# Inverse deviations of the norms by a logarithm and an exponential on ScalarE in place of a power on GpSimd, in a four-layer graph network kernel

## The chip, the cores and the metric

The kernel runs on one core of a Trainium2 chip. A core has five engines that run side by side, each with its own in-order queue of instructions: TensorE (PE, matrix products; its weight loads are shown apart as PEld), VectorE (DVE), ScalarE (ACT), GpSimd (POOL) and SyncE (SP), which here issues the DMAs. The metric is the device time of one execution in microseconds (us), lower is better. A profile page and the answers of the trace come from one profiled execution.

## The reference, cut to what matters

The input `x` is 32 batches of 512 nodes with 128 features; `adj` is a 512 x 512 adjacency matrix of zeros and ones. Four graph layers follow each other, each as a residual around a layer norm without weights:

```python
def _layernorm(x, axis=-1, eps=1e-5):
    m = jnp.mean(x, axis=axis, keepdims=True)
    v = jnp.var(x, axis=axis, keepdims=True)
    return (x - m) / jnp.sqrt(v + eps)

h = jnp.maximum(_layernorm(x), 0.0); x = x + layer0(h, adj)   # pair attention
h = jnp.maximum(_layernorm(x), 0.0); x = x + layer1(h, adj)   # attention, norm, adjacency sum, MLP with a norm
h = jnp.maximum(_layernorm(x), 0.0); x = x + layer2(h, adj)   # attention, elu
h = jnp.maximum(_layernorm(x), 0.0); x = x + layer3(h, adj)   # softmax of a learned adjacency
return x
```

So each batch needs six norms: one ahead of each layer and two inside layer 1 (one after its attention, one in its MLP). Every norm needs one inverse deviation, 1/sqrt(v + eps), for each of the 512 nodes. The 512 nodes lie as 4 chunks of 128 partitions, so that the inverse deviations of one norm are a 128 x 4 tile. 32 batches make 192 norms.

## The kernel before

**How the work is cut.** The unit is one batch in one layer, a 128 x 4 x 128 tile in float32. `xs` holds `x` for all batches in on-chip memory from load to store. `layer0(b)` to `layer3(b)` record the operations of one batch: the norm (`preln`), a projection, attention scores, and products that accumulate in PSUM banks. All matrix work is float32 on PE.

**What sets the order.** The kernel doesn't issue instructions as it records them. Each operation is handed to a planner (`Plan`) with its engine, an estimated length in us and the values that it reads and writes. Each batch in each layer is a chain with a due time: the layers of successive batches start at the distances `GAPS`, and layers 1, 2 and 3 of a batch follow 6, 12 and 16 batches behind layer 0 (`LAGS`). `Plan.run` then goes through all operations once, always takes the one that can begin first by the estimated lengths (ties within 0.05 us go to the earlier due time), and emits it. The order that comes out is fixed for each engine. So a change to the engine or length of one kind of operation moves the order of all engines.

**Idle products.** Where the planner finds PE without work for more than 0.6 us and a PSUM bank is free, it emits dummy transposes of the identity matrix, one for every 0.11 us of the gap beyond 0.2 us (`idle_products`, L334). They keep PE busy and compute nothing that is used. The program before has 150 of them.

**A norm, step by step.** `variances` (L511, L513, VectorE) gives mean and variance, `mv`. `inv_dev` gives `rstd`: on GpSimd, `ve = mv + eps` (L523), then `ve` to the power -0.5 (L525). Ahead of layer 0 of the first eight batches (`EARLY`) the normalized tile `xn` is made on ScalarE (L545); in all other norms ahead of a layer it is made on GpSimd in four pieces (L560), with the negated mean, `shift`, from ScalarE (L556). PE turns `xn` into `pt` (L421), and ScalarE copies that to `hT` with the ReLU (L570). In layer 1 the norm after the attention takes its power at L892 from a `ve` that VectorE makes (L883), and VectorE uses it in `hn` (L899); the norm of the MLP uses `inv_dev`, and ScalarE scales `zn` by it (L927).

**Small tiles** (`mv`, `rstd`, `shift` and the like) come from the pool `sm` with eight buffers for each name.

**DMA.** SP issues the loads of `x` (L405), the rearranged scores `u` of layer 0 (L699) and the stores of the result (L992), in the planner's order.

The power itself is two lines:

```python
nc.gpsimd.tensor_scalar(ve, mv.own[:, :, 1], LN_EPS, 1.0, ALU.add, ALU.mult)
nc.gpsimd.tensor_tensor(rstd.own, ve, mhalf, ALU.pow)
```

Of the kernel before, what the change touches and what calls it, by code (L numbers as in the profile page):

```python
# [28 lines left out]
F32 = mybir.dt.float32  # L29
# [4 lines left out]
AF = mybir.ActivationFunctionType  # L34
ALU = mybir.AluOpType
# [9 lines left out]
OLD, KEPT = 4, 1  # L45

AHEAD = 6


PE, DVE, ACT, POOL, SP = "PE", "DVE", "ACT", "POOL", "SP"  # L50
# [207 lines left out]
def kernel(  # L258
# [33 lines left out]
    P2 = P + 2  # L292
    NE = l3_e.shape[1]
    KE = NE // P
    assert F == P and C == 4 and NE % P == 0 and B >= AHEAD

    cp = ctx.enter_context(tc.tile_pool(name="const", bufs=1))
    ps = ctx.enter_context(tc.tile_pool(name="ps", bufs=8, space=bass.MemoryType.PSUM))
    sm = ctx.enter_context(tc.tile_pool(name="sm", bufs=8))

    def wide(t):

# [4 lines left out]

    def small(name, shape=(P, C)):
        return sm.tile(list(shape), F32, name=name, tag=name)

    def const(name, shape, dtype=F32):
        return cp.tile(list(shape), dtype, name=name)
# [40 lines left out]
    nc.vector.memset(mhalf, -0.5)  # L353
    minus1 = const("minus1", (P, 1))
    nc.vector.memset(minus1, -1.0)
    one_b = const("one_b", (P, 1), BF16)
    nc.vector.memset(one_b, 1.0)


    xs = const("xs", (P, B, C, P))  # L360
    W_S, W_2, W_30, W_31 = range(4)
    wts = const("wts", (P, 4, P))
    att = const("att", (P, 2))
# [30 lines left out]
    def row_of(n):  # L394
        return rows[:, n : n + 1, :].to_broadcast([P, C, P])

    v_x = [Value() for _ in range(B)]
    v_adj = [Value() for _ in range(C)]
    v_adjT = [Value() for _ in range(C)]
    v_biasT, v_mask2T, v_cnt, v_w0, v_wts = Value(), Value(), Value(), Value(), [Value() for _ in range(4)]  # L400
# [3 lines left out]
    def load(dst, src, writes, size=0.0):  # L404
        op(SP, 0.5, lambda: nc.sync.dma_start(dst(), src), writes=writes, load=size, transfers=1)  # L405

    def load_x(b):
        load(lambda: xs[:, b], x[b].rearrange("(c p) f -> p c f", p=P), [v_x[b]], 1.0)

    def copy_op(engine, length, dst, src, reads, writes):  # L410
        if engine is ACT:
# [88 lines left out]
    def dve(length, emit, reads, writes, port=0):  # L500
        op(DVE, length, emit, reads, writes, port=port)

    def variances(src, reads):

        mv = Value()

        def emit():
            st = small("st", (P, C, 6))
            mv.own = small("mv", (P, C, 2))
            for c in range(C):  # L510
                nc.vector.bn_stats(st[:, c, :], src(c))  # L511
            for c in range(C):
                nc.vector.bn_aggr(mv.own[:, c, :], st[:, c, :])  # L513

        dve(1.1, emit, reads, [mv])
        return mv

    def inv_dev(mv):
        rstd = Value()

        def emit():
            ve = small("ve")
            nc.gpsimd.tensor_scalar(ve, mv.own[:, :, 1], LN_EPS, 1.0, ALU.add, ALU.mult)  # L523
            rstd.own = small("rstd")
            nc.gpsimd.tensor_tensor(rstd.own, ve, mhalf, ALU.pow)  # L525

        op(POOL, 1.3, emit, [mv], [rstd])
        return rstd

    def preln(b, engine):  # L530

        src = xs[:, b]
        mv = variances(lambda c: src[:, c, :], [v_x[b]])
        rstd = inv_dev(mv)
        shift = Value()
        xn = value(by_act if engine is ACT else by_pool, "xn")
        if engine is ACT:

            def emit_shift():
                shift.own = small("shift")  # L540
                nc.vector.scalar_tensor_tensor(shift.own, mv.own[:, :, 0], -1.0, rstd.own, ALU.mult, ALU.mult)

            def norm():
                for c in range(C):
                    nc.scalar.activation(  # L545
                        xn.t[:, c, :], src[:, c, :], AF.Identity, bias=shift.own[:, c : c + 1],
                        scale=rstd.own[:, c : c + 1],
                    )

            dve(0.08, emit_shift, [mv, rstd], [shift], port=1)  # L550
            op(ACT, 1.54, norm, [shift, rstd, v_x[b]], [xn])
        else:

            def emit_shift():
                shift.own = small("shift")
                nc.scalar.mul(shift.own, mv.own[:, :, 0], -1.0)  # L556

            def norm():
                for c in range(C):
                    nc.gpsimd.tensor_scalar(  # L560
                        xn.t[:, c, :], src[:, c, :], shift.own[:, c : c + 1], rstd.own[:, c : c + 1],
                        ALU.add, ALU.mult,
                    )

            op(ACT, 0.1, emit_shift, [mv], [shift])
            op(POOL, 1.72, norm, [shift, rstd, v_x[b]], [xn], port=4)
        pt = value(banks, "pt")
        turn_op(lambda k: pt.t[:, k, :], lambda k: xn.t[:, k, :], [xn], [pt])
        hT = value(by_act, "hT")
        op(ACT, 0.49, lambda: nc.scalar.activation(wide(hT.t), wide(pt.t), AF.Relu), [pt], [hT])  # L570
        return hT, pt
# [115 lines left out]
    def layer0(b):  # L687
# [138 lines left out]
        def terms():  # L826
            return second[0].t.rearrange("p (c t) f -> p c t f", c=H)

        for ib in range(C):
# [20 lines left out]
               [hT, v_wts[W_S], *([*y, hs] if ib < H else [v_mask2T, *hi, *lo])], [po[ib]])  # L850
        rest = value(by_act, "rest")
        op(ACT, 0.27, lambda: nc.scalar.copy(rest.t[:, 0:H, :], terms()[:, :, 1, :]), second, [rest])
        dve(0.33, lambda: nc.vector.tensor_add(xs[:, b, 0:H, :], xs[:, b, 0:H, :], first[0].t[:, 0:H, :]),
            first, [v_x[b]])
        dve(0.33, lambda: nc.vector.tensor_add(xs[:, b, H:, :], xs[:, b, H:, :], terms()[:, :, 0, :]),
            second, [v_x[b]])
        op(POOL, 0.7, lambda: nc.gpsimd.tensor_add(xs[:, b, H:, :], xs[:, b, H:, :], rest.t[:, 0:H, :]),
           [rest], [v_x[b]], port=1)


    def layer1(b):
# [23 lines left out]
        dve(0.08, emit_q, ssum, [q], port=1)  # L885
        mv = variances(lambda c: po[0].t[:, c, :], po)
        dve(0.08, emit_ve, [q, mv], [ve], port=1)
        rr = Value()

        def emit_rr():  # L890
            rr.own = small("rstd")
            nc.gpsimd.tensor_tensor(rr.own, ve.own, mhalf, ALU.pow)  # L892

        op(POOL, 1.0, emit_rr, [ve], [rr])
        hn = value(by_dve, "hn")

        def emit_hn():
# [27 lines left out]
        def emit_zn():  # L925
# [9 lines left out]
        px = project(zT, wts[:, W_2, :], [v_wts[W_2]], "px")  # L935
        res = value(by_dve, "res")
        op(DVE, 0.6, lambda: nc.vector.tensor_add(res.t, px.t, hgb.t), [px, hgb], [res])
        op(DVE, 0.6, lambda: nc.vector.scalar_tensor_tensor(xs[:, b], res.t, 0.0, xs[:, b], ALU.max, ALU.add),
           [res], [v_x[b]], port=1)


    def layer2(b):
        hT, _ = preln(b, POOL)
        h = project_scored(hT, w2_ext, [v_w2])
        po, ssum = attend(h, lambda: h[0].t[:, :, P], h, h, None, None)
        v1 = value(by_dve, "v1")

        rs = Value()

        def emit_rs():  # L950
            rs.own = small("rs")
            nc.vector.reciprocal(rs.own, ssum[0].own)

        dve(0.1, emit_rs, ssum, [rs])
        dve(0.6, lambda: nc.vector.tensor_mul(v1.t, po[0].t, per_chunk(rs.own)), [*po, rs], [v1])  # L955
        op(POOL, 1.25, lambda: nc.gpsimd.tensor_add(v1.t, v1.t, row_of(B_L2)), [v_rows], [v1], port=1)  # L956


        em = value(by_act, "em")
        op(ACT, 0.62, lambda: nc.scalar.activation(em.t, v1.t, AF.Exp, bias=minus1), [v1], [em])  # L960
        op(DVE, 0.6, lambda: nc.vector.scalar_tensor_tensor(em.t, em.t, 1.0, v1.t, ALU.min, ALU.max), [v1], [em], port=1)  # L961
        op(POOL, 1.25, lambda: nc.gpsimd.tensor_add(xs[:, b], xs[:, b], em.t), [em], [v_x[b]], port=1)  # L962


    def layer3(b):
        hT, pt = preln(b, POOL)

        own = value(by_dve, "own")
        op(DVE, 0.6, lambda: nc.vector.scalar_tensor_tensor(wide(own.t), wide(pt.t), 0.0, adiag_rep, ALU.max, ALU.mult),
           [pt, v_adiag_rep], [own])  # L970
        xb = value(by_pool, "xb")
        op(POOL, 1.25, lambda: nc.gpsimd.tensor_add(xb.t, xs[:, b], row_of(B_L3)), [v_x[b], v_rows], [xb], port=1)
        p1 = project(hT, wts[:, W_31, :], [v_wts[W_31]], "p1")
        h1 = value(by_act, "h1")
        copy_op(ACT, 0.49, lambda: h1.t, lambda: p1.t, [p1], [h1])
        po = parts(banks, "po", C)
        for ib in range(C):

            def emit_po(ib=ib):
                nc.tensor.matmul(  # L980
                    po[ib].t[:, ib, :], lhsT=own.t[:, ib, :], rhs=wts[:, W_30, :], start=True, stop=False
                )
                for jb in range(C):
                    nc.tensor.matmul(  # L984
                        po[ib].t[:, ib, :], lhsT=offT[:, jb, blk(ib)], rhs=h1.t[:, jb, :],
                        start=False, stop=(jb == C - 1),
                    )

            op(PE, 1.11, emit_po, [own, h1, v_offT, v_wts[W_30]], [po[ib]])
        yo = value(by_dve, "yo")  # L990
        op(DVE, 0.6, lambda: nc.vector.tensor_add(yo.t, xb.t, po[0].t), [xb, *po], [yo])
        op(SP, 0.5, lambda: nc.sync.dma_start(out[b].rearrange("(c p) f -> p c f", p=P), yo.t), [yo], [Value()], load=1.0, transfers=1)  # L992
# [369 lines left out]
```

## Time and profile before

| | |
|---|---|
| time, median of 3 runs | 1062.31 us (1062.3 to 1063.7) |
| span of the profiled execution | 1062.1 us |
| mean clock granted to TensorE | 0.996 of full speed |
| power on GpSimd in `inv_dev` (L525) | 160 instructions, 170.9 us busy |
| the addition ahead of it (L523) | 160 instructions, 38.3 us busy |
| power of the norm after the attention (L892) | 32 instructions, 33.6 us busy |
| idle products on PE (L334) | 150 instructions, 19.2 us busy |
| activation table loads on ScalarE | 1, 1.3 us |

How to read the views: the page gives the busy time of each engine and its share of the span. A busy share is an average over stages, so the views by stretch of time give the same for windows that begin and end at chosen microseconds. The chain of waits is followed back from the last instruction: at each step to what released it, or else to the instruction before it on its engine. A group line gives the source line, engine, operation, tiles (out<-in), shape, count, busy time, mean duration in ns, and then the idle time of the engine just before, with what ended it. One float32 product of the source is two PE instructions in the profile; where such instructions follow each other closely their durations overlap, so that a row's busy time can be less than its count times its mean.

### The profile page before, as it was taken

What the parts mean: (1) busy time and instruction counts of PE and PEld (TensorE: products, weight loads), DVE (VectorE), ACT (ScalarE), POOL (GpSimd) and SP (SyncE); (2) the same over time, 40 slices, a digit from 0 to 9 for tenths busy, and PEclk for the clock granted to TensorE, in tenths of its full rate; (3) what the DMA queues carried; (4) which work ended last, traced back from release to release, by engine and by line L of the source; (5) the groups of instructions that cost most, each with busy time, mean ns of one, the idle gap of its engine ahead of it and who ended that gap; (6) DMA issues with size and microseconds to landing.
All of it is one profiled execution on the core that took longest, in us unless ns stands there. A gap on an engine that the chain in (4) does not pass through costs nothing.

```text
span 1062.1 us, 25166 instructions
## 1 busy us (share of the span) xinstructions
PE 1041.7 (98%) x8475; PEld 966.0 (91%) x8475; DVE 868.5 (82%) x3694; ACT 780.5 (73%) x2024; POOL 776.2 (73%) x1140
## 2 busy tenths in 40 slices
PE   7899999999999999999999999999999999999998
PEld 7789789989999999999999999999899999999997
DVE  7799999989988878888888888888888877766752
ACT  6768897789877777777877777787777777767751
POOL 4489577778787777787778778777877666576772
PEclk9899999999999999999999999999999999999999
DMA  6400000000010000000000000000000000000001
GB/s 181 96 12 2 1 2 21 2 12 11 2 31 2 21 21 21 22 21 12 2 12 11 12 12 12 11 2 11 12 11 11 11 11 11 11 22 11 22 24 37
DMA packets 56912, 20.49 MB, mean 19 GB/s; under 512 B 21584, under 2 KB 56272, under 8 KB 56784
## 3 DMA queue, kind: packets, MB, share of 16 engines
q1 hardware_dynamic: 56784, 18.90, 7.2%
q8 instruction: 67, 1.10, 0.5%
q14 instruction: 61, 0.50, 0.2%
HBM read 10.43 MB, written 8.39 MB: 18 GB/s over the span
## 4 chain that ended last, share of the span: by engine, by line
PE 88%; DVE 4%; POOL 3%; DMA 1%; SPq 1%; issue 1%; ACT 1%; POOLq 0%; DVEq 0%; ACTq 0%
PE po L675 20%; PE pt L421 16%; PE po L984 10%; PE pg L911 10%; PE proj L595 7%; PE po L837 5%; PE prow L421 3%; PE p L581 3%; PE pz L581 3%; PE px L581 3%; PE po L980 3%; PE po L842 2%; PE po L834 1%; PE po L847 1%; POOL xn L560 1%
## 5 line engine op out<-in xcount | busy, mean ns | idle before, releaser
L675 PE MATMUL po<-h,pT 128*128 128x128 f32 x2048 | 242.8, 275 | 0.8 <-DVE pT L664 0.8
L675 PEld LDWEIGHTS po<-h,pT 128*128 128x128 f32 x2048 | 236.4, 192 | 5.8 <-issue 4.1
L560 POOL TENSOR_SCALAR xn<-xs,shift,rstd 128x128 f32<-128x128 f32 x480 | 213.1, 459 | 2.8 <-DVE top L633 0.9
L655 ACT ACTIVATE y<-y,nmax 128x512 f32<-128x512 f32 x256 | 181.7, 714 | 5.3 <-DVE nmax L637 4.6
L525 POOL TENSOR_TENSOR rstd<-ve,mhalf 128x4 f32<-128x4 f32 x160 | 170.9, 1068 | 13.3
L622 DVE CUSTOM_DVE_ANT_0 y<-prow,bias 128x512 f32<-128x512 f32 x256 | 162.8, 683 | 1.6 <-PE prow L421 1.6
L984 PE MATMUL po<-h,offT 128*128 128x128 f32 x1024 | 135.4, 275 | 0.0
L911 PE MATMUL pg<-adjTe,hg 128*128 128x512 f32 x256 | 131.0, 593 | 0.0
L421 PE MATMUL pt<-ident,y 128*128 128x128 f32 x1024 | 130.2, 274 | 0.7 <-ACT hl L819 0.7
L421 PEld LDWEIGHTS pt<-ident,y 128*128 128x128 f32 x1024 | 115.1, 141 | 13.8 <-issue 8.5
L984 PEld LDWEIGHTS po<-h,offT 128*128 128x128 f32 x1024 | 124.6, 192 | 0.0
L511 DVE BATCH_NORM_STATS2 st<-xs 128x6 f32<-128x128 f32 x512 | 109.8, 277 | 7.2 <-POOL xs L962 4.5
L595 PEld LDWEIGHTS proj<-w_ext,hT 128*128 128x128 f32 x768 | 96.8, 192 | 19.0 <-issue 9.6
L595 PE MATMUL proj<-w_ext,hT 128*128 128x130 f32 x768 | 102.9, 277 | 1.4 <-ACT hT L570 1.3
L647 ACT ACTIVATE y<-y,src 128x512 f32<-128x512 f32 x128 | 84.6, 714 | 20.8 <-DVE rmax L622 19.6
L962 POOL TENSOR_TENSOR xs<-xs,em 128x512 f32<-128x512 f32 x32 | 42.0, 1312 | 76.8 <-DVE em L961 63.8
L956 POOL TENSOR_TENSOR v<-v,rows 128x512 f32<-128x512 f32 x32 | 40.9, 1279 | 72.4 <-DVE v L955 72.4
L570 ACT ACTIVATE hT<-pt 128x512 f32<-128x512 f32 x128 | 73.5, 589 | 25.3 <-PE pt L421 14.0
L647 ACT ACTIVATE y<-y,h 128x512 f32<-128x512 f32 x128 | 84.7, 714 | 7.9 <-DVE rmax L622 7.7
L664 DVE TENSOR_TENSOR pT<-pt,adjT 128x512 f32<-128x512 f32 x128 | 82.6, 681 | 5.7 <-PE pt L421 5.6
L421 PE MATMUL pt<-ident,xn 128*128 128x128 f32 x512 | 77.8, 274 | 1.5 <-POOL xn L560 1.3
L412 ACT COPY h<-proj 128x260 f32<-128x260 f32 x192 | 66.1, 371 | 13.4 <-PE proj L595 12.4
(204 smaller groups left out, 2302.3 us busy)
## 6 DMA issues: line engine op xcount, KB each, us to landing
xs<-in_x_dram SPq DMA_DIRECT2D x32, 256.0 KB, 4.0
out_dram<-yo SPq DMA_DIRECT2D x32, 256.0 KB, 2.3
u<-h SPq DMA_DIRECT2D x128, 0.5 KB, 1.8
bias<-in_adj_dram SPq DMA_DIRECT2D x4, 256.0 KB, 4.4
wts<-in_L_gnn_W_dram SPq DMA_DIRECT2D x3, 64.0 KB, 4.2
rows<-in_L_gnn_bias_dram SPq DMA_DIRECT2D x2, 64.0 KB, 3.7
wt_o<-L_gnn_others_weight_dram SPq DMA_DIRECT2D x1, 64.0 KB, 2.5
wts<-n_L_gnn_self_weight_dram SPq DMA_DIRECT2D x1, 64.0 KB, 4.5
```

Of the source, the lines that this page charges most:

```text
L421: nc.tensor.transpose(dst(k), src(k), ident)
L511: nc.vector.bn_stats(st[:, c, :], src(c))
L525: nc.gpsimd.tensor_tensor(rstd.own, ve, mhalf, ALU.pow)
L560: nc.gpsimd.tensor_scalar(xn.t[:, c, :], src[:, c, :], shift.own[:, c : c + 1], rstd.own[:, c : c + 1], ALU.add, ALU.mult,)
L581: nc.tensor.matmul(pt.t[:, c, :], lhsT=column(hT, c), rhs=w, start=True, stop=True)
L595: nc.tensor.matmul(p[:, c, :], lhsT=column(hT, 2 * k + c), rhs=w_ext, start=True, stop=True)
L622: nc.vector.tensor_tensor_reduce(wide(y[ib].t), wide(prow.t), bias[:, ib, :], 1.0, LOWEST, ALU.add, ALU.max, rmax.own[:, ib : ib + 1],)
L647: nc.scalar.activation(yw, yw, AF.Prelu, alpha=0.2, bias=src()[:, ib : ib + 1])
L655: nc.scalar.activation(yw, yw, AF.Exp, bias=nmax.own[:, ib : ib + 1], accum_out=ssum[0].own[:, ib : ib + 1])
L675: nc.tensor.matmul(po[ib].t[:, ib, :], lhsT=pT.t[:, jb, :], rhs=h[0].t[:, jb, 0:P], start=(jb == 0), stop=(jb == C - 1),)
L911: nc.tensor.matmul(wide(pg.t), lhsT=hg.t[:, nb, :], rhs=adjTe[:, nb, :], start=(nb == 0), stop=(nb == C - 1))
L984: nc.tensor.matmul(po[ib].t[:, ib, :], lhsT=offT[:, jb, blk(ib)], rhs=h1.t[:, jb, :], start=False, stop=(jb == C - 1),)
```

## The change

The inverse deviation becomes exp(-0.5 * ln(v + eps)) on ScalarE in 184 of the 192 norms: the 152 norms of `inv_dev` outside the first eight of layer 0, and the 32 norms after the attention of layer 1. The first eight norms of layer 0, whose `xn` is made on ScalarE, keep the power on GpSimd. The table set that holds both functions is loaded ahead of the work. `mv`, `rstd`, `shift` and the new `log` tile come from a new pool `sn` with 24 buffers for each name. `xs` holds 26 batches in place of 32, and the last six batches use the room of the first six again.

```diff
+HELD = 26
...
+    sn = ctx.enter_context(tc.tile_pool(name="sn", bufs=24))
...
+    eps_ln = const("eps_ln", (P, 1))
+    nc.vector.memset(eps_ln, LN_EPS)
+    nc.scalar.preload_act_table_set("natural_log_exp_and_others")
...
-    xs = const("xs", (P, B, C, P))
+    xs = const("xs", (P, HELD, C, P))
...
-    v_x = [Value() for _ in range(B)]
+    v_x = [Value() for _ in range(HELD)] * 2
...
-        load(lambda: xs[:, b], x[b].rearrange("(c p) f -> p c f", p=P), [v_x[b]], 1.0)
+        load(lambda: xs[:, b % HELD], x[b].rearrange("(c p) f -> p c f", p=P), [v_x[b]], 1.0)
...
-            mv.own = small("mv", (P, C, 2))
+            mv.own = lasting("mv", (P, C, 2))
...
-    def inv_dev(mv):
+    def inv_root(var, reads, bias=None):
+
+        log, rstd = Value(), Value()
+
+        def emit_log():
+            log.own = lasting("log")
+            if bias is None:
+                nc.scalar.activation(log.own, var(), AF.Ln)
+            else:
+                nc.scalar.activation(log.own, var(), AF.Ln, bias=bias)
+
+        def emit_root():
+            rstd.own = lasting("rstd")
+            nc.scalar.activation(rstd.own, log.own, AF.Exp, scale=-0.5)
+
+        op(ACT, 0.2, emit_log, reads, [log])
+        op(ACT, 0.2, emit_root, [log], [rstd])
+        return rstd
+
+    def inv_dev(mv, engine=ACT):
+        if engine is ACT:
+            return inv_root(lambda: mv.own[:, :, 1], [mv], eps_ln)
         rstd = Value()
...
-        rstd = inv_dev(mv)
+        rstd = inv_dev(mv, POOL if engine is ACT else ACT)
...
-        rr = Value()
-
-        def emit_rr():
-            rr.own = small("rstd")
-            nc.gpsimd.tensor_tensor(rr.own, ve.own, mhalf, ALU.pow)
-
-        op(POOL, 1.0, emit_rr, [ve], [rr])
+        rr = inv_root(lambda: ve.own, [ve])
...
```

More of the change, by code (lines that the diff above doesn't have):

```diff
@@ L294 @@
     KE = NE // P
-    assert F == P and C == 4 and NE % P == 0 and B >= AHEAD
+    assert F == P and C == 4 and NE % P == 0 and AHEAD <= B <= 2 * HELD
     cp = ctx.enter_context(tc.tile_pool(name="const", bufs=1))
@@ L309, in small, with lasting @@
         return sm.tile(list(shape), F32, name=name, tag=name)
+    def lasting(name, shape=(P, C)):
+        return sn.tile(list(shape), F32, name=name, tag=name)
     def const(name, shape, dtype=F32):
@@ L523, in emit @@
             nc.gpsimd.tensor_scalar(ve, mv.own[:, :, 1], LN_EPS, 1.0, ALU.add, ALU.mult)
-            rstd.own = small("rstd")
+            rstd.own = lasting("rstd")
             nc.gpsimd.tensor_tensor(rstd.own, ve, mhalf, ALU.pow)
@@ L530, in preln @@
     def preln(b, engine):
-        src = xs[:, b]
+        src = xs[:, b % HELD]
         mv = variances(lambda c: src[:, c, :], [v_x[b]])
-        rstd = inv_dev(mv)
+        rstd = inv_dev(mv, POOL if engine is ACT else ACT)
         shift = Value()
@@ L539, in emit_shift @@
             def emit_shift():
-                shift.own = small("shift")
+                shift.own = lasting("shift")
                 nc.vector.scalar_tensor_tensor(shift.own, mv.own[:, :, 0], -1.0, rstd.own, ALU.mult, ALU.mult)
@@ L554, in emit_shift @@
             def emit_shift():
-                shift.own = small("shift")
+                shift.own = lasting("shift")
                 nc.scalar.mul(shift.own, mv.own[:, :, 0], -1.0)
@@ L852, in layer0 @@
         op(ACT, 0.27, lambda: nc.scalar.copy(rest.t[:, 0:H, :], terms()[:, :, 1, :]), second, [rest])
-        dve(0.33, lambda: nc.vector.tensor_add(xs[:, b, 0:H, :], xs[:, b, 0:H, :], first[0].t[:, 0:H, :]),
+        dve(0.33, lambda: nc.vector.tensor_add(xs[:, b % HELD, 0:H, :], xs[:, b % HELD, 0:H, :], first[0].t[:, 0:H, :]),
             first, [v_x[b]])
-        dve(0.33, lambda: nc.vector.tensor_add(xs[:, b, H:, :], xs[:, b, H:, :], terms()[:, :, 0, :]),
+        dve(0.33, lambda: nc.vector.tensor_add(xs[:, b % HELD, H:, :], xs[:, b % HELD, H:, :], terms()[:, :, 0, :]),
             second, [v_x[b]])
-        op(POOL, 0.7, lambda: nc.gpsimd.tensor_add(xs[:, b, H:, :], xs[:, b, H:, :], rest.t[:, 0:H, :]),
+        op(POOL, 0.7, lambda: nc.gpsimd.tensor_add(xs[:, b % HELD, H:, :], xs[:, b % HELD, H:, :], rest.t[:, 0:H, :]),
            [rest], [v_x[b]], port=1)
@@ L937, in layer1 @@
         op(DVE, 0.6, lambda: nc.vector.tensor_add(res.t, px.t, hgb.t), [px, hgb], [res])
-        op(DVE, 0.6, lambda: nc.vector.scalar_tensor_tensor(xs[:, b], res.t, 0.0, xs[:, b], ALU.max, ALU.add),
+        op(DVE, 0.6, lambda: nc.vector.scalar_tensor_tensor(xs[:, b % HELD], res.t, 0.0, xs[:, b % HELD], ALU.max, ALU.add),
            [res], [v_x[b]], port=1)
@@ L961, in layer2 @@
         op(DVE, 0.6, lambda: nc.vector.scalar_tensor_tensor(em.t, em.t, 1.0, v1.t, ALU.min, ALU.max), [v1], [em], port=1)
-        op(POOL, 1.25, lambda: nc.gpsimd.tensor_add(xs[:, b], xs[:, b], em.t), [em], [v_x[b]], port=1)
+        op(POOL, 1.25, lambda: nc.gpsimd.tensor_add(xs[:, b % HELD], xs[:, b % HELD], em.t), [em], [v_x[b]], port=1)
     def layer3(b):
@@ L971, in layer3 @@
         xb = value(by_pool, "xb")
-        op(POOL, 1.25, lambda: nc.gpsimd.tensor_add(xb.t, xs[:, b], row_of(B_L3)), [v_x[b], v_rows], [xb], port=1)
+        op(POOL, 1.25, lambda: nc.gpsimd.tensor_add(xb.t, xs[:, b % HELD], row_of(B_L3)), [v_x[b], v_rows], [xb], port=1)
         p1 = project(hT, wts[:, W_31, :], [v_wts[W_31]], "p1")
```

## The prediction

> **What bounds the kernel now.** I read the busy times first, then the chain of waits as shares, then the busy times by stretch, then the chain and the instructions inside the stretches where PE isn't full.
>
> From the page, the busy time of each engine and the chain's shares:
>
> ```profile
> PE 1041.7 (98%) x8475; PEld 966.0 (91%) x8475; DVE 868.5 (82%) x3694; ACT 780.5 (73%) x2024; POOL 776.2 (73%) x1140
> ...
> PE 88%; DVE 4%; POOL 3%; DMA 1%; SPq 1%; issue 1%; ACT 1%; POOLq 0%; DVEq 0%; ACTq 0%
> ```
>
> GpSimd, which the change relieves, holds 3% of the chain; PE holds 88%. By stretch (length, busy time of each engine):
>
> ```profile
> 55.00:74.50 19.50, 17.93 (x148) 16.18 (x148) 18.39 (x88) 10.46 (x38) 16.83 (x26) 1.00 0.05 2
> 74.50:125.40 50.90, 48.86 (x382) 45.03 (x383) 47.93 (x207) 43.31 (x119) 42.86 (x62) 1.00 0.04 7
> 125.40:200.00 74.60, 74.60 (x580) 66.69 (x581) 71.24 (x328) 62.39 (x173) 53.94 (x75) 1.00 0.05 9
> 200.00:985.00 785.00, 784.84 (x6416) 727.56 (x6416) 649.83 (x2692) 591.09 (x1506) 593.35 (x867) 1.00 0.05 13
> 985.00:1062.00 77.00, 71.02 (x624) 69.39 (x622) 39.47 (x122) 35.90 (x79) 42.86 (x63) 0.99 0.08 25
> ```
>
> The reader should see that from 125.4 to 985 us PE is idle for 0.16 us in all. That PE isn't merely shown as busy but issues at its own pace follows from the chain, where 32 instructions of L675 take 3.57 us every time, 112 ns each. A faster norm can't shorten those 860 us. What it can shorten is the filling of the pipeline up to 125 us and the emptying after 985.
>
> The chain inside the filling (start, length, what):
>
> ```profile
> 58.02 1.02 POOL rstd L525
> ...
> 67.90 1.02 POOL rstd L525
> ...
> 71.56 2.87 POOL xn L560 x4
> ...
> 89.28 1.27 DVE pT L664 x2
> ```
>
> From 57 to 74.5 the chain lies on GpSimd and passes through its powers; from about 81 to 125 it lies mostly on DVE, and after that on PE.
>
> **The change, part by part.** *What leaves GpSimd.* By the group rows a power takes 1.07 us and its addition 0.24 us. 152 of 160 leave L525 (162.4 us) and L523 (36.4), and all 32 of L892 (33.6): 232 us of 776. GpSimd falls to about 51% of the span. None of it is gain where PE is full. In 57.7 to 74.5 four powers (4.18 us) and four additions (1.22) go, 5.4 us of the 16.11 that GpSimd is busy there.
>
> *What ScalarE gets.* 184 logarithms and 184 exponentials of 128x4. Nearest rows:
>
> ```profile
> L765 ACT ACTIVATE e<-ltn 128x4 f32<-128x4 f32 x32 | 6.2, 195 | 0.2 <-DVE ltn L754 0.2
> ...
> L556 ACT ACTIVATE shift<-mv 128x4 f32<-128x4 f32 x120 | 23.0, 205 | 48.3 <-DVE mv L513 25.7 <-DVE rsum L791 9.9 <-POOL xn L560 9.6
> ```
>
> An exponential of this size exists: 195 ns. No logarithm does; from below it costs the same 195 ns. From above: 152 of them take their bias from a tile, as L960 does, which needs 720 ns for 512 elements where the plain copy L412 needs 587, so 133 more, 328 ns. I take the upper end, since L960 is the row with that operand: 152 x 0.328 + 32 x 0.195 + 184 x 0.195 = 92 us, at the lower end 72 us. ScalarE goes from 780.5 to between 852 and 873 us, at most 82%. In the full stretch it is busy 591 of 785 us, so a batch period of 31.14 us (L675 recurs at 507.75 and 538.89) has 7.7 us free, of which twelve small instructions use 2.3 to 3.0. I cost that at nothing: the cover is ScalarE's idle time, a quarter of the stretch. Without it, 2.3 to 3.0 us would come onto each of about 27 periods.
>
> [...]
>
> *The table load.* The trace has one load of 1.28 us, and the built program of the changed kernel has one, too, only earlier. It is covered by the first DMAs, for which PE waits until 3.91 us. If the set switched in every norm, 368 loads of 1.28 us would be 472 us.
>
> *What is queued behind the new waits.* A logarithm waits for `mv` in ScalarE's in-order queue; behind it stand the copies `h`, `hT` and `pT` that feed PE. The row of `shift`, which waits for the same `mv`, prices this: 25.7 us in 29 waits, 0.89 us each, in 29 of 120 cases. Six logarithms a period with that frequency are 1.3 us, beside 3.0 us of work still under the 7.7 free. The MLP's norm loses a crossing: ScalarE waited 6.0 us for GpSimd's `rstd` at L927.
>
> *The filling.* The four powers and additions on the chain, 5.4 us, go; the pair on ScalarE lies beside GpSimd, which has other work, and ScalarE is idle 9 of the 19.5 us from 55 on. What is late next is DVE: from 57.7 to 74.5 it is busy 16.66 of 16.8 us, and to 125.4 another 47.93 of 50.9, so 3.1 us of room for compressing the same work. The changed program's order, known before it runs, is the same on PE up to row 121 (about 55 us) and then has 20 idle products in the filling where there were 41. A product advances the chain by 110 ns (34 in 3.73 us): 21 x 0.11 = 2.3 us. Between 2.3 and 3.1 I take 2.5. Bounds: PE's idle time from 55 to 125.4, 1.57 + 2.04 us, and all 41 products, 4.5 us, make 8.1 at best; below nothing, since the new order may leave as many short waits as the old, 3.6 us more at worst, less the products, +1.3.
>
> *The emptying.* The last norm of all shows it:
>
> ```profile
> 1046.33 0.20 POOL L523 TENSOR_SCALAR ve<-mv 128x4 f32<-128x4 f32 x1
> ...
> 1046.61 1.02 POOL L525 TENSOR_TENSOR rstd<-ve,mhalf 128x4 f32<-128x4 f32 x1
> 1047.73 1.74 POOL L560 TENSOR_SCALAR xn<-xs,shift,rstd 128x128 f32<-128x128 f32 x4
> ...
> 1048.75 0.93 PE L334 MATMUL idle<-ident 128*128 128x128 f32 x7
> ```
>
> PE runs seven dummies while this `xn` is late. Addition and power last from 1046.33 to 1047.63, 1.3 us; logarithm and exponential are 0.33 + 0.20 and a hand-over, 0.6 to 0.8. The changed order lacks just these seven: 0.8 us. Two more waits for a norm at 998.9 and 1020.0 (0.39 and 0.52 us) may shrink; I add 0.2. So 1.0. Bounds: 19 products (2.1) and the gaps ahead of the last matmul (5.98 less the 4.1 us behind it, 1.9), so 4.0 at best and nothing at worst.
>
> *The rest.* Reusing `xs`: the reload of a slot stands behind the store of its old batch in SP's queue, which had waited for the last reader already, and six batches (187 us) ahead of its use: nothing; were it late, DVE's `st` and so PE would wait the 4.0 us that a load takes. The pool of 24 buffers only takes waits away. `eps_ln` is one memset under the first DMA.
>
> Sum: 2.5 + 1.0 = 3.5 us off the profiled 1062.1, so 1058.6; the median lies 0.2 above that execution's span: **1058.8 us**.
>
> **The rivals.** *More than the planner shows* (0.10): GpSimd held the whole filling, and PE then has no idle time in it. All of 8.1 + 4.0: 1050.2 us; for it, the chain of 57 to 74.5; against it, DVE, as full as GpSimd in the same stretch.
>
> *Hidden anyway* (0.17): DVE limits the filling so closely that short waits return what the idle products gave, and the end gains at most 0.8: 1061.5 to 1062.3 us. For it, the chain on DVE from 81 to 125; against it, 4.5 us of dummies that the stretch before has.
>
> *Slower* (0.12): ScalarE's queue becomes the bound of the full stretch. The point is 7.7 us a period: 3.0 us of new work and a wait of 0.89 us for every one of six logarithms (5.3) is 8.3, 0.6 over. A delay of 0.3 us in each of 27 periods already takes 8.1, less the gain of 3.5: 1066.9 us; the full 0.6 gives 1075. Against it: only a quarter of the `shift` waits ended idle time.
>
> *A table load in each norm* (0.01): 1534 us.
>
> **How the numbers follow.** The forecast has 0.60. The range 1053.0 to 1064.5 goes from three quarters of the best case to a delay of about 0.2 us a period; outside lie 0.06 below and 0.12 above. A measurement here tells 0.2% (2.1 us) from no change. Faster by more: most of the forecast (0.58), the best case (0.10) and a little of the hidden one (0.02), 0.70; slower: 0.13; the rest, 0.17, within.
>
> **What would show it.** Right: GpSimd near 51%, ScalarE near 81%, logarithms of 195 to 328 ns; PE without idle time from about 125 to 985 us; idle products 20 in the filling and 12 at the end; the chain at 57 to 75 us no longer on GpSimd. Wrong: idle time on PE in the middle ended by ScalarE, more than one table load, or waits in the filling that sum to more than 3.6 us.

## The result, and the profile after

The change made the kernel slower: 1072.38 us in the median of four executions (1068.75 to 1073.37) against 1062.30 of before beside it (1061.67 to 1063.70). The ratio is 1.0088, with a 95% interval of 1.0070 to 1.0106. The forecast was 1058.8 us, with a range of 1053.0 to 1064.5.

The profiled execution has a span of 1067.0 us, 4.9 over the one of before. It is the fastest of its four (1068.75 us; a time is about 1.7 us more than its span), and the profiled one of before was the slowest of its four, so the two profiles show only half of the 10 us between the medians. A later run of the same kernel shows more of it (experiment 10).

From the page of the changed kernel: the busy time, share and instructions of each engine, then the engines' shares of the chain that ended last, and the group row of the logarithm (busy time and mean ns of one after the bar):

```profile
PE 1038.0 (97%) x8447; PEld 958.9 (90%) x8447; DVE 871.8 (82%) x3695; ACT 829.2 (78%) x2392; POOL 550.8 (52%) x804
...
PE 87%; DVE 6%; ACT 4%; DMA 1%; SPq 1%; issue 1%; POOL 0%; DVEq 0%; POOLq 0%; ACTq 0%
...
L535 ACT ACTIVATE log<-mv,eps_ln 128x4 f32<-128x4 f32 x152 | 44.6, 298 | 49.7 <-DVE nmax L779 28.9
```

GpSimd went from 776 to 551 us and left the chain, as meant. PE is busy for 3.7 us less although the span grew (3.6 us of that are idle products left out): the time was lost in front of PE. The busy time by stretch of the changed kernel, in the same columns and stretches as before, says where:

```profile
55.00:74.50 19.50, 18.06 (x145) 16.37 (x146) 17.18 (x78) 11.71 (x42) 19.50 (x37) 1.00 0.09 16
74.50:125.40 50.90, 39.67 (x280) 34.91 (x279) 44.15 (x186) 38.62 (x114) 24.16 (x34) 0.90 0.02 1
125.40:200.00 74.60, 74.08 (x578) 66.02 (x577) 70.81 (x323) 63.05 (x190) 33.31 (x46) 1.00 0.04 9
200.00:985.00 785.00, 783.49 (x6391) 723.11 (x6391) 652.24 (x2699) 630.63 (x1811) 413.71 (x596) 1.00 0.05 13
985.00:1067.00 82.00, 77.43 (x690) 76.71 (x688) 42.04 (x136) 43.70 (x106) 38.36 (x56) 0.99 0.09 27
```

In the second row PE works for 39.67 of 50.90 us, where it was 48.86 before, and the granted clock is 0.90 instead of 1.00. From 125 to 985 us, which is most of the kernel, PE lost 2 us in all. The end is shorter. The waits of PE, summed over the span (what waited, for what; us in total, times, longest), lead to the place:

```profile
PE po L863 <- ACT h L420: 6.0, 1, 6.0
...
PE prow L429 <- DVE src L897: 3.9, 1, 3.9
```

These are two single waits, and the timeline of PE (start, length, what, then the idle time before it and what ended it) shows that they follow each other:

```profile
74.72 0.61 PE L624 MATMUL proj<-w_ext,hT 128*128 128x130 f32 x4
79.22 1.08 PE L429 MATMUL prow<-ident,ls 128*128 128x128 f32 x4 [3.90 <-DVE src L897]
86.28 0.79 PE L863 MATMUL po<-wts,hT 128*128 128x128 f32 x2 [5.97 <-ACT h L420]
86.86 1.91 PE L866 MATMUL po<-hs,y 128*128 128x128 f32 x8
```

From 75.3 to 86.3 us PE does one thing, for 1.1 us. No idle product stands there. The first of the two waits is for an operand, `ls`, which VectorE makes one instruction ahead of `src`:

```profile
78.92 0.15 DVE L741 SCALAR_TENSOR_TENSOR ls<-sc 128x4 f32<-128x4 f32 x1
```

VectorE is busy nearly all the time (3.97 of 4.00 us from 75 to 79); from 75.74 to 78.79 the variances of two younger norms (L519, L521) stand ahead of `ls` in its queue. The third line of PE is the one to read closely. Its operands are `wts` and `hT`; `h`, whose copy ended the wait, is not among them. What the copy L420 does for L863 is to empty a PSUM bank: the product had its operands and no bank to write to (by the planner's estimated times it was ready at 75.3 us and its bank came free at 81.2). The timeline of ScalarE says why that copy was late:

```profile
72.14 0.60 ACT L599 ACTIVATE hT<-pt 128x512 f32<-128x512 f32 x1 [2.66 <-PE pt L429]
75.42 0.37 ACT L881 COPY rest<-po 128x256 f32<-128x256 f32 x1 [2.68 <-DVE xs L884]
...
77.82 1.65 ACT L574 ACTIVATE xn<-xs,shift,rstd 128x128 f32<-128x128 f32 x4
79.38 1.93 ACT L676 ACTIVATE y<-y,src 128x512 f32<-128x512 f32 x3
...
85.87 0.62 ACT L420 COPY h<-proj 128x260 f32<-128x260 f32 x2
```

ScalarE itself sat idle twice for 2.7 us up to 75.4 us and then worked without a gap until the copy at 85.87, mostly on the attention of older chains. None of the logarithms and exponentials of the norms (L533, L535, L539) is executed from 75.4 to 86.3: the new instructions are not what held the bank. What did is the order. The planner's own bookkeeping, in estimated times, reads as follows. From about 70 to 81 us seven of the eight banks belong to young chains (batches that had just entered a layer). The eighth, which `KEPT` holds back for the older ones, goes at 74.0 us to the `prow` of an older chain, and the next product of another older chain then has none. The projection that holds the wanted bank could not be copied out, because five of the six tiles `scored`, into which such copies go, were held by older chains, and the sixth is held back by `KEPT` as well. A tile came free at 75.9 us; from then to 80.7 the copy, being of a younger chain, stood behind the work of older chains on ScalarE. An idle product needs a free bank beyond the one that the next product takes, so that the longest gap of the kernel is one that has none.

The account of PE, in us, for these and for the experiments below (PE idle is length less busy time; work is PE's busy time without idle products):

| kernel | idle to 55 | 55 to 125.4 | 125.4 to 985 | after 985 | idle products | work | span |
|---|---|---|---|---|---|---|---|
| before | 10.5 | 3.6 | 0.2 | 6.1 | 19.2 | 1022.5 | 1062.1 |
| changed | 9.7 | 12.7 | 2.0 | 4.6 | 15.7 | 1022.4 | 1067.0 |
| 1: order of before, pair on ScalarE | 9.9 | 3.6 | 3.4 | 5.8 | 19.2 | 1023.8 | 1065.8 |
| 3: rest only | 10.3 | 3.4 | 0.5 | 6.1 | 19.2 | 1019.3 | 1058.7 |
| 4: changed, 8 `scored` | 10.1 | 6.6 | 1.6 | 4.2 | 16.2 | 1021.9 | 1060.6 |
| 5: before, one length | 11.7 | 6.8 | 2.7 | 4.7 | 18.1 | 1024.8 | 1068.7 |
| 6: changed, 8 `scored`, 10 powers | 9.3 | 11.3 | 2.7 | 4.2 | 18.1 | 1024.1 | 1069.6 |
| 7: changed, 14 powers | 8.7 | 5.0 | 3.7 | 4.2 | 18.3 | 1021.2 | 1061.1 |
| 10: changed once more | 9.0 | 12.8 | 2.2 | 4.6 | 15.7 | 1024.6 | 1068.8 |

Of the changed kernel's 4.9 us, +9.1 arose from 55 to 125 us, +1.9 in the middle, -0.8 ahead, -1.5 at the end, -3.6 in idle products left out, and -0.1 in the work itself.

### The profile page after: what moved, and what is told of

The parts are those of the page before. It is cut to its first block, busy times and chain, and to the rows that moved or that the text cites. A ratio compares the mean times of both kernels' runs of the same rounds, so it can differ in the third digit from the quotient of the medians.

```text
span 1067.0 us, 24978 instructions
## 1 busy us (share of the span) xinstructions
PE 1038.0 (97%) x8447; PEld 958.9 (90%) x8447; DVE 871.8 (82%) x3695; ACT 829.2 (78%) x2392; POOL 550.8 (52%) x804
## 4 chain that ended last, share of the span: by engine, by line
PE 87%; DVE 6%; ACT 4%; DMA 1%; SPq 1%; issue 1%; POOL 0%; DVEq 0%; POOLq 0%; ACTq 0%
PE po L704 20%; PE pt L429 16%; PE po L1007 11%; PE pg L934 10%; PE proj L624 7%; PE po L866 4%; PE prow L429 3%; PE po L1003 3%; PE px L610 3%; PE p L610 3%; PE pz L610 3%; PE po L871 2%; PE po L863 1%; PE po L876 1%; DVE st L519 1%; PE idle L339 1%
## 5 line engine op out<-in xcount | busy, mean ns | idle before, releaser
L704 PE MATMUL po<-h,pT 128*128 128x128 f32 x2048 | 240.2, 275 | 0.3 <-DVE pT L693 0.3
L519 DVE BATCH_NORM_STATS2 st<-xs 128x6 f32<-128x128 f32 x512 | 110.1, 275 | 9.2 <-POOL xs L985 6.6
L849 POOL TENSOR_TENSOR hl<-hs,hl 128x256 fp32r<-128x256 f32 x64 | 46.1, 742 | 99.3 <-ACT hl L848 99.3
L599 ACT ACTIVATE hT<-pt 128x512 f32<-128x512 f32 x128 | 75.3, 590 | 16.7 <-PE pt L429 15.8
L535 ACT ACTIVATE log<-mv,eps_ln 128x4 f32<-128x4 f32 x152 | 44.6, 298 | 49.7 <-DVE nmax L779 28.9
L420 ACT COPY h<-proj 128x260 f32<-128x260 f32 x192 | 65.3, 372 | 22.0 <-PE proj L624 20.3
```

The lines of the kernel that those rows point to most:

```text
L704: nc.tensor.matmul(po[ib].t[:, ib, :], lhsT=pT.t[:, jb, :], rhs=h[0].t[:, jb, 0:P], start=(jb == 0), stop=(jb == C - 1),)
```

## The experiments

The expectations speak of two theories. The order theory: the planner's new order lets young chains hold the PSUM banks in the filling. The ScalarE theory: the 368 small instructions delay ScalarE's other work.

**1. The order of before, the pair on ScalarE.** The planner sees the kernel of before; at the power's place logarithm and exponential are issued on ScalarE.

```diff
-            nc.gpsimd.tensor_tensor(rr.own, ve.own, mhalf, ALU.pow)
+            log = small("log")
+            nc.scalar.activation(log, ve.own, AF.Ln)
+            nc.scalar.activation(rr.own, log, AF.Exp, scale=-0.5)
```

(and likewise in `inv_dev`)

> The kernel before, whose planner still reckons with a power on GpSimd (1.3 and 1.0 us), so that its order stays; but where it would emit the power, logarithm and exponential go to ScalarE's queue (184 norms). Order theory (the time is lost because the planner's new order in the filling lets young chains hold the PSUM banks): 1058 to 1063 us, no single wait of PE over 2 us between 55 and 125 us. ScalarE theory (the 368 small instructions themselves delay the copies that feed PE): 1067 to 1074 us.

Measured: 1067.37 us (1066.81 to 1069.4), ratio 1.0049 (1.0035 to 1.0062). The time is the one that the ScalarE theory had expected, 4 us above the range of the order theory. But there is no hole (the long waits of PE of the changed kernel near 75 to 86 us): beyond the start no wait of PE exceeds 1.6 us. The busy times from 74.5 and from 200 us in this run:

```profile
74.50:125.40 50.90, 48.43 (x375) 44.01 (x375) 49.43 (x206) 44.32 (x132) 32.62 (x47) 1.00 0.02 2
...
200.00:985.00 785.00, 783.26 (x6385) 724.08 (x6384) 654.78 (x2683) 642.72 (x1797) 416.32 (x595) 1.00 0.05 13
```

The filling is as full as before, but PE idles 3.4 us from 125 to 985 in place of 0.2, in short waits, none over 0.6 us, most of them ended by ScalarE (`y`, `hT`, `zT`, `h`). So the ScalarE theory has a part here: pairs that the planner did not reckon with cost this order about 5 us in the median, though ScalarE is idle for a fifth of the time.

**2. The order of the change, addition and power on GpSimd.** The planner sees the changed kernel; what is issued at the pair's places runs on GpSimd.

```diff
-            nc.scalar.activation(rstd.own, log.own, AF.Exp, scale=-0.5)
+            nc.gpsimd.tensor_tensor(rstd.own, log.own, mhalf, ALU.pow)
```

> The changed kernel, whose planner reckons with two steps of 0.2 us on ScalarE; but in their places addition and power are emitted on GpSimd, so that the order stays the changed kernel's and ScalarE gets none of the new work. Order theory: 1067 to 1080 us, with PE waits of some 10 us near 75 to 86 us. ScalarE theory: back to 1060 to 1064 us.

Measured: 1143.83 us (1141.23 to 1146.44), ratio 1.0770. That is far outside both expectations. As a time it tells little: the powers stand where the plan has no room for them on GpSimd, and PE idles all along (36.9 us from 125 to 985). But the waits of PE in this run still have the hole:

```profile
PE pt L429 <- ACT y L683: 12.0, 17, 1.8
PE pt L429 <- POOL xn L588: 11.7, 8, 4.1
PE po L862 <- ACT h L420: 6.6, 1, 6.6
```

The 6.6 us wait for the bank is there without a logarithm on ScalarE, later than in the changed kernel (it ends at 98.9 us), and again a wait of 3.2 us for `prow` stands ahead of it. It goes with the order.

**3. The rest of the change alone.** All powers stay on GpSimd; the reuse of `xs`, the pool of 24 and the early table load remain.

```diff
-    def inv_dev(mv, engine=ACT):
+    def inv_dev(mv, engine=POOL):
...
-        rr = inv_root(lambda: ve.own, [ve])
+        op(POOL, 1.0, emit_rr, [ve], [rr])
```

> The changed kernel's smaller xs with its reuse, its pool of 24 buffers and its early table load, but every inverse deviation by the power on GpSimd, planned as before. Order and ScalarE theory both: 1061 to 1064 us, as before. If the reuse of xs or the pool costs the time: 1067 us or more.

Measured: 1060.87 us (1060.06 to 1063.24), ratio 0.9989 (0.9980 to 0.9998). The side edits cost nothing. The profiled execution (1058.7 us) is short beyond that: by the account its idle time is that of before, its work 3.3 us less. Its clock was full around 50 us (1.00 in the mean from 0 to 55), where that of before was granted half (0.50 from 48 to 52).

**4. Two more tiles for the copies.**

```diff
-    scored = room("scored", 6, (P, C, P2))
+    scored = room("scored", 8, (P, C, P2))
```

> The changed kernel with 8 instead of 6 tiles for the copied projections (scored), nothing else. Order theory with PSUM banks as its means (projections sit in PSUM because no tile to copy them to is free): the waits of PE near 75 to 86 us shrink from 9.9 us to under 5, 1064 to 1069 us. ScalarE theory: no change, 1069 to 1073 us.

Measured: 1061.61 us (1060.25 to 1062.29), ratio 0.9991 (0.9982 to 0.9999): 10.8 us below the changed kernel, with all of its pairs on ScalarE. That rules out the ScalarE theory's 1069 to 1073, and it is more than the order theory had expected (1064 to 1069). The stretch of the hole, in this run:

```profile
74.50:125.40 50.90, 46.23 (x357) 41.85 (x357) 48.17 (x217) 43.08 (x129) 28.50 (x42) 1.00 0.03 7
```

PE is busy for 6.6 us more than in the changed kernel there, at full clock, and no wait of PE there is over 1.7 us. ScalarE's 368 extra instructions, where the planner reckons with them, leave 1.6 us of idle PE from 125 to 985 us.

**5. The same instructions as before, another order.** The kernel of before with one estimated length altered; no instruction that computes a result is added, removed or moved to another engine. Only the idle products, which the planner places, go from 150 to 143.

```diff
-        op(POOL, 1.3, emit, [mv], [rstd])
+        op(POOL, 1.25, emit, [mv], [rstd])
```

> The kernel before with every instruction as it was; only the length that the planner reckons for addition and power is 1.25 us instead of 1.3. Order theory (a greedy order that can fill the PSUM banks with young chains, whatever moves it): the order of the filling changes, PE has waits of 2 to 6 us between 70 and 90 us, each ended by the engine that copies a bank out, and the kernel takes 1064 to 1069 us. ScalarE theory: no logarithm, so 1061 to 1064 us.

Measured: 1070.27 us (1069.14 to 1072.03), ratio 1.0068 (1.0056 to 1.0081), 1.3 us above what the order theory had expected. The wait is the same one, though 3.0 us long (the line numbers are those of the kernel before, L834 for L863), and PE's timeline after it reads the same:

```profile
90.87 0.80 PE L834 MATMUL po<-wts,hT 128*128 128x128 f32 x2 [2.99 <-ACT h L412]
91.46 1.92 PE L837 MATMUL po<-hs,y 128*128 128x128 f32 x8
93.16 0.63 PE L834 MATMUL po<-wts,hT 128*128 128x128 f32 x2
93.59 1.91 PE L837 MATMUL po<-hs,y 128*128 128x128 f32 x8
```

0.05 us in an estimate costs 7.4 us, three quarters of what the whole change does, with neither a logarithm nor an exponential for a norm. The hole isn't all of it. Of the 6.6 us between this profile and that of before, +3.2 are idle time in the filling, +2.5 idle time in the middle, +2.3 longer work (the clock is 0.95 from 55 to 125 us), +1.2 idle time ahead, -1.4 at the end and -1.1 idle products. Run 4 idles as much in the filling (6.6 us) and takes 1061.6. So an edit that moves the plan can put that much at stake without touching the work.

**6 and 7. Power kept in more of the first norms.** With `b < 10` and eight `scored` tiles (6), and with `b < 14` and six (7):

```diff
-        rstd = inv_dev(mv, POOL if engine is ACT else ACT)
+        rstd = inv_dev(mv, POOL if b < 14 else ACT)
```

> The changed kernel with 8 tiles for copied projections, as in s4, and the norms of the first ten batches ahead of all four layers by the power on GpSimd, so with some 26 fewer pairs on ScalarE in and near the filling. Order theory: the order turns over once more; here transposed tiles (pt) of young chains wait in PSUM for other tiles than scored, so PE waits 8 to 12 us near 75 to 90 us again: 1068 to 1074 us. ScalarE theory: less work for ScalarE in the filling than in s4, so at most 1062 us.

> The changed kernel (6 tiles for copied projections), with the power on GpSimd in the norms ahead of all layers for the first fourteen batches. Order theory: no PE wait over 2 us between 55 and 125 us, 1057 to 1062 us; the full stretch is as in the changed kernel. ScalarE theory: the filling is freed of logarithms, the rest is not; if they cost in the full stretch too, 1064 us or more.

Run 6 gave 1071.56 us (1071.22 to 1073.87), ratio 1.0087 (1.0074 to 1.0101), as the order theory had expected, though with fewer pairs on ScalarE than run 4. Eight tiles don't rule the hole out; its one wait is the longest of all:

```profile
PE po L863 <- ACT h L420: 9.1, 1, 9.1
```

It is once more the wait for the copy of a projection, so the transposed tiles (`pt`) that the expectation named aren't what this product waited for.

Run 7 gave 1062.76 us (1060.72 to 1063.88), ratio 0.9998 (0.9989 to 1.0006), with six tiles and no wait of PE over 1.6 us beyond the start; it lies 0.8 us above the order theory's range and under the 1064 of the ScalarE theory. So neither the tiles nor the powers are a cure in themselves; each edit makes another order. The orders with the long wait for a bank took 1070 to 1073 us (the changed kernel, 5, 6; run 2, whose powers have no room, apart). Those without it took 1061 to 1063 (before, 3, 4, 7, and 8 and 9 below), except run 1, whose pairs the planner didn't reckon with.

**8. A retuned version, meant to beat both.** Eight tiles, `b < 12`, lengths of 0.16 for the pair, `RAMP` 4.0, `EARLY` 6, first gap 5.2.

```diff
-RAMP = 4.1
+RAMP = 4.0
...
-EARLY = 8
+EARLY = 6
...
-        op(ACT, 0.2, emit_log, reads, [log])
-        op(ACT, 0.2, emit_root, [log], [rstd])
+        op(ACT, 0.16, emit_log, reads, [log])
+        op(ACT, 0.16, emit_root, [log], [rstd])
```

> The changed kernel with its order retuned: power for the first twelve batches ahead of the layers, 8 tiles for copied projections, RAMP 4.0, EARLY 6, first of GAPS 5.2, 0.16 us reckoned for logarithm and exponential. Order theory: no PE wait over 2 us between 55 and 125 us, 1055 to 1061 us, faster than both kernels. ScalarE theory: not under 1062 us.

Measured: 1063.24 us (1061.67 to 1064.27), ratio 1.0000 (0.9992 to 1.0009). A miss of the order theory's 1055 to 1061: it has no wait of PE over 2 us and is level with before, and so are runs 4 and 7 within 0.1%.

**9. Control for 4.** The kernel of run 3 with eight `scored` tiles.

> Control for s4: every power stays on GpSimd (the kernel of s3), with 8 in place of 6 'scored' tiles. Order theory: s3 has no hole in the filling, so two more tiles have nothing to close: no PE wait over 2 us but the start, 1058.5 to 1063 us, ratio 0.997 to 1.001, level with s3 and s4. If 8 tiles are worth something by themselves (so that s4's gain over the changed kernel is not the closing of its hole), this run is at least 3 us below s3's 1060.9: under 1058 us, ratio under 0.996.

Measured: 1062.70 us (1061.44 to 1064.29), ratio 0.9997 (0.9989 to 1.0006). The tiles are worth nothing where there is no hole, so the 10.8 us of run 4 are not what the tiles give by themselves; they came with an order that has no hole.

**10. The changed kernel once more.**

> The changed kernel itself once more, for the place and the size of its hole. Order theory: the order is fixed, so the wait of L863 for the copy h out of a PSUM bank stands in this profile too, 5 to 7 us between 79 and 87 us, with 8-pass groups near 1.9 us behind it; 1068 to 1074 us, ratio 1.006 to 1.011. ScalarE theory: if the loss were chance delays by ScalarE, the longest wait of PE in the filling would lie elsewhere or be under 3 us, with the loss spread over 125 to 985 us.

Measured: 1072.58 us (1070.58 to 1075.02), ratio 1.0094 (1.0079 to 1.0109). Its waits of PE:

```profile
PE po L863 <- ACT h L420: 6.4, 1, 6.4
...
PE prow L429 <- DVE src L897: 3.9, 1, 3.9
```

The hole is the same. This profiled span is 1068.8 us: 1.8 over the first, with nearly equal idle time (28.6 and 29.0 us) and 2.2 us more of PE work. From 0 to 55 us its granted clock is 0.97, like run 5's and midway between before's 0.94 and the 1.00 of the first profile; and behind the hole its clock stayed at half for about 4.4 us of work (0.50 from 90 to 92 us, 1.00 from 92 to 94), against 2.9 in the first. Estimated from these, 3% of the 46 us of work up to 55 and half of the 1.5 us behind the hole are 2.1 us, which fits the 2.2. So the first profile of the changed kernel had the more favourable clock; with run 10 the loss reads 6.7 us. What the slower executions of the changed kernel, up to 1075 us, add to that was not profiled and stays open.

## Why the prediction was wrong

*The step that failed is the filling*, -2.5 us with a bound of +1.3 on the bad side. The prediction counted the idle products of the changed order, 20 where there were 41, and read the missing 21 as PE waits that had vanished. The count was right (20, and 2.6 us of busy time less), the reading wrong: the planner issues idle products only where a bank is free. A gap for want of a bank has none, so fewer of them can also mean worse gaps; and runs 6 and 5 have 39 and 41 of them in the filling, with the hole all the same. PE's other idle time went from 3.6 to 12.7 us where at most 3.6 more had been allowed for; the sign said by the prediction to show it wrong, waits in the filling of more than 3.6 us in sum, is what came.

*The rival on the slow side* had the right sign and, with 1066.9 to 1075 us, the right size, but its mechanism is not what was seen: it put the loss into the full stretch, by ScalarE's queue. From 125 to 985 us PE lost 1.9 of the rival's 8 us, and run 4 shows the full stretch at 1.6 us with every pair in it. Run 5, which has no pair, idles 2.7 us there, so that even those 2 us aren't shown to be the pairs'. That the new order might hold up PSUM was not among the rivals.

*ScalarE's work.* The logarithm took 298 ns with the bias from a tile and 213 without, the exponential 205: inside 195 to 328. ScalarE went to 829 us, not to between 852 and 873. The three rows sum to 88.1 us of busy time, but neighbours on ScalarE overlap (one exponential of 0.19 us starts at 740.16, the next instruction at 740.25), and the total grew by 48.7. The difference is 107 ns for each of the 368, an overlap which the prediction left out. How much overlaps depends on the order: in run 1 nearly the same rows (88.3 us) raised the total by 65.5. The term was too high by the overlap, to no effect. Costing it at nothing held to about 2 us where the planner reckons with it (change and run 4; 3.7 us in run 7), and not in run 1, where the cover, ScalarE's idle fifth, was there and PE lost 3.2 us more in the middle all the same: an average of idle time doesn't say that each copy for PE is on time.

*GpSimd* came to 52% (51% forecast), and the chain at 57 to 75 us is no longer on it. *The emptying*, -1.0 us: PE idles 1.5 us less after 985, and the seven idle products are gone; `xn` starts 0.67 us after the last `mv` row where it was 1.50, as the 0.6 to 0.8 of the prediction had it. That the gain at the end comes from it isn't shown, and two runs speak against it: run 5, with the power, idles 4.7 us there and has the same 12 idle products, while run 1, with the pair and the order of before, idles 5.8 and keeps 19. By these the end goes with the order, and that the sign came true was partly luck. *The table load* is one, of 1.28 us, for all 184 logarithms and 184 exponentials. *The rest*, `xs` and the pools: nothing, by run 3.

*The gain was small in any case.* Without the hole, the change gives 0.9982 to 1.0006 of the time before (runs 4 and 7): the 225 us taken off GpSimd lay beside a PE that is full for 860 us. Several signs that the prediction named for being right (GpSimd near 51%, the logarithm's length, the 20 and 12 idle products) came true in a kernel that got slower: they tell that the change was made, not that it pays.

## What to carry to other kernels

Where a scheduler decides the order, an edit has two effects, that of its instructions and that of the new order, and the second can be the larger. Alter one estimated length without touching an instruction, and see how far the time swings, before an edit is credited or blamed. When a wait ends on an instruction whose result the waiting one doesn't read, look for the buffer that it frees, and for who holds the others; but check first that it isn't merely the neighbour of an operand's maker, as `src` was of `ls`. A filler that needs the scarce resource itself is no measure of the gaps.

## What the runs showed of the hardware

The granted clock of PE went to a half and back, within a window of half a microsecond each time (0.94 from 78.5 to 79 us and 0.50 from 79; 0.82 from 89 to 89.5, 0.50 ahead of it and 1.00 behind). In the changed kernel (length, then the busy times, and the clock behind them):

```profile
75.00:79.00 4.00, 0.33 (x3) 0.13 (x2) 3.97 (x25) 3.58 (x14) 4.00 (x10) 0.99 0.00 0
79.00:83.00 4.00, 1.08 (x4) 0.71 (x4) 4.00 (x20) 4.00 (x9) 1.74 (x3) 0.50 0.00 0
...
86.00:88.00 2.00, 1.73 (x8) 1.73 (x9) 0.77 (x2) 1.26 (x8) 2.00 (x3) 0.50 0.00 0
...
90.00:93.00 3.00, 2.92 (x27) 2.71 (x26) 1.67 (x10) 2.39 (x9) 2.03 (x3) 1.00 0.00 0
```

After a wait of 3.9 us the clock was 0.50, and it was full again at about 89.2, 2.9 us after work had begun at 86.3 (from the share of 0.71 between 88 and 90 us). In between, eight passes of L866 took 1.91 us, where they take 1.06 at full clock (at 69.50 and 70.61 us; the clock is 1.00 from 55 to 74.5); 2.9 us at half speed are about 1.4 us lost behind the wait. In run 5 the clock fell in the wait of 3.0 us, after shorter ones (0.87 from 88 to 90 us, 0.50 from 90 to 92), and about 5.4 us of work ran at half clock (0.50 from 94 to 96, 0.93 from 96 to 98); in run 10, the changed kernel again, it was about 4.4 us of work. So the profiles show two levels, half and full, and a change of place between two executions of one kernel (2.9 and 4.4 us). They show no one length of idle time ahead of a fall: the clock fell in waits of 3.9 and of 3.0 us; in run 10 it was still full after a wait of 3.9 us and fell in the next, at about 81.8 (from the share of 0.85 between 79 and 83 us); and in the profile of before it fell at about 47 us, where PE had worked 1.99 of the 4.00 us from 44 to 48. Why the half-clock stretch around 50 us is present in the profile of before and absent from that of run 3 no run here shows.
